# Fixed expert blocks, an adding scatter, and the first blocks beside the last batch's routing

## The chip, the cores and the metric

The kernel runs on one core of one Trainium2 chip. The metric is the device time of one execution in microseconds, and lower is better. A core has five engines that work side by side, each in the order of its own instructions: TensorE (PE, matrix products), VectorE (DVE), ScalarE (ACT), GpSimd (POOL) and SyncE (SP, which here only issues transfers). Transfers run on 16 DMA engines that all queues share. An engine waits for another, or for a transfer, through semaphores, and everything behind a waiting instruction on the same engine waits too.

## The reference

The input `x` is 4 images of 32 x 32 positions with 256 channels, so 4 batches of 1024 tokens. Layer 0 is a convolution with a selective scan. Layer 1 is an attention without a softmax over tokens, followed by a mixture of 16 experts, of which each token takes two:

```
t = tokens(layer0(x))
t = t + attn(layernorm(t))
xe = layernorm(t)                                  # 4096 x 256
probs = softmax(xe @ gate_w + gate_b)              # 16 experts
top_probs, top_idx = top_k(probs, 2); top_probs /= sum(top_probs)
hidden = silu(xe @ w1[e]) * (xe @ w2[e])           # 256 -> 512
t = t + sum over the two experts e:  top_prob * (hidden @ w3[e])   # 512 -> 256
```

The reference computes every expert for every token and weights most of them with zero. The kernel computes only the two that count.

## The kernel before, in words

**Layer 0** (to line 1159) takes most of the time: a scan over 64 states for each of 4 batches, with all engines busy. The change does not touch it.

**Attention** (lines 1221 to 1742) runs batch by batch in an order written out by hand. The iteration for batch `o` multiplies out its attention, prepares the keys and queries of batch `o + 1`, and does the routing of batch `o - 1`. The routing is a generator, `route`, whose steps are small DVE operations; `on_with(steps, n)` puts the next `n` of them at a given place in the order. For the last batch nothing follows to run its routing beside, so lines 1730 to 1742 put it at the end: `turn_e` turns the normalised tokens `xe`, `gates` multiplies them by the gate weights, `turn_g` turns the result back, and `route` picks the two experts, counts for each token how many earlier tokens chose the same expert, and writes the one-hot matrices `qh` of the place in a block. The tokens themselves are written to a DRAM tensor `xd` by `expert_in`. They stay in SBUF too, in `t_all`.

**Blocks.** The expert stage works on blocks of 128 (token, choice) pairs that share one expert. Lines 1748 to 1825 lay the blocks out once all four batches are routed: each expert gets the number of blocks that its count needs, one expert after the other. `eid` holds the expert of each block, `src` the row of `xd` for each place of each block, and `dst` the row of the output list. To find `src` and `dst`, each of 64 groups of 128 pairs is multiplied (bf16) by a matrix that marks its block.

**The expert stage** (lines 1830 to 1931) runs `NFULL` = 74 blocks, and more only under a condition on the number that is used. For each block, `fetch_in` reads the expert number into a register on SP and loads `w1` and `w2` (0.5 MB each), `fetch_out` loads `w3` (0.5 MB), both four blocks ahead, and POOL gathers 128 rows of `xd` with an indirect transfer. `turn_rows` transposes the rows on PE, `hidden` computes half of the hidden layer into PSUM (tile `p12`, four buffers), SiLU on ACT, the product on DVE, and `result` multiplies by `w3`. `put_result` copies the block's result to `yb` (four buffers) and POOL scatters it with an indirect transfer to `yd`, a DRAM list with one row for each (token, choice) pair. POOL's queue therefore alternates gathers and scatters.

**The end** (lines 1934 to 1947). Because the two results of a token lie in two rows of `yd`, the last loop loads all of `yd` (8 loads of 1 MB), multiplies each row by its weight `wts`, adds it to `t_all` on DVE, and stores the output from ACT's queue.

The lines that set the order at the border and in a block:

```
            hidden(i, 0)                    # lines 1917 to 1925, for each block i
            result(i - 1, 2); put_result(i - 1)
            turn_rows(i + 1)
            hidden(i, 2)
            result(i, 0)
```

Of the kernel before, what the change touches and what calls it, by code (L numbers as in the profile page):

```python
# [8 lines left out]
F32 = mybir.dt.float32  # L9
# [7 lines left out]
P = 128  # L17
BANK = 512

BS = P  # L20
# [13 lines left out]
def conv_ssm_attn_moe_kernel(ctx: ExitStack, tc: tile.TileContext, a: dict, out: bass.AP):  # L34
# [19 lines left out]
    NBLK = 2 * NB * L // BS + NE - 1  # L54
    assert 2 * NS == P
# [1112 lines left out]
    wts = l1.tile([P, 2, NTA], F32, name="wts")  # L1168

    t_all = l1.tile([P, NTA, C], F32, name="t_all")  # L1170
    xd = dram.tile([NB * L, C], F32, name="xd")

    yd = dram.tile([2 * NB * L + P, C], F32, name="yd")
# [4 lines left out]
    groups_f = l1.tile([P, NTA], F32, name="groups_f")  # L1178

    places = l1.tile([P, BS], BF16, name="places")  # L1180
    blocks_h = l1.tile([P, NBLK], BF16, name="blocks_h")

    groups = l1.tile([P, NTA], BF16, name="groups")
    part_pk = l1.tile([P, 2], F32, name="part_pk")
    spare = l1.tile([P, 1], F32, name="spare")
# [7 lines left out]
    counts = [l1.tile([P, NE], F32, name=f"counts{b}") for b in range(NB)]  # L1193
    within = l1.tile([P, 2, NTA], F32, name="within")
    qh = l1.tile([P, 2, NTA, BS], BF16, name="qh")

    def constants(first):
        def count(t, n, lo, step=1, across=0):
            nc.gpsimd.iota(
                t, [[step, n]], base=lo, channel_multiplier=across,  # L1200
                allow_small_or_imprecise_dtypes=True,
            )

        if first:
            count(iota, NE, NE)
            make_upper_triangular(nc, before, 1.0, diag=False)
            count(places_f, BS, 0)
            count(blocks, NBLK, 0)
            count(groups_f, NTA, 0)
            count(part_pk, 2, 1, 1, 2)  # L1210
            count(spare, 1, 2 * NB * L + 1, 1, 1)
            count(block_p, 1, 0, 1, 1)
        else:
            nc.vector.memset(every, 1.0)
            nc.vector.memset(keep, 1.0)
            nc.vector.memset(keep[:, :, 0:1], 0.0)
            nc.vector.tensor_copy(places, places_f)
            nc.vector.tensor_copy(blocks_h, blocks)
            nc.vector.tensor_copy(groups, groups_f)

    with tc.tile_pool(name="wa", bufs=1) as wa, tc.tile_pool(name="att", bufs=1) as att, \
            tc.tile_pool(name="sm", bufs=2) as sm, \
            tc.tile_pool(name="ps_b", bufs=2, space=PSUM) as ps_b, \
            tc.manual_schedule():
        HT = NT // 2
        tbs = [t_all[:, b * NT : (b + 1) * NT, :] for b in range(NB)]
        for i in (0, HT):
            nc.sync.dma_start(out=tbs[0][:, i : i + HT, :], in_=rows(td, 0)[:, i : i + HT, :])
        for b in range(1, NB - 1):
            nc.sync.dma_start(out=tbs[b], in_=rows(td, b))  # L1230
        nc.sync.dma_start(out=tbs[-1][:, TPB:, :], in_=rows(xf, NB - 1)[:, TPB:, :])
        nc.sync.dma_start(out=tbs[-1][:, :TPB, :], in_=rows(td, NB - 1)[:, :TPB, :])
        wg = load_rows("L1_ffn_gate_w", CK, NE, wa)
        gb = load_bcast("L1_ffn_gate_b", NE, wa)
        wqk, wvo, bqk, bvo, bout = made["mats"]

        batch = [{} for _ in range(NB)]

        def stat(on, kind, x, i, n=NT):

            if i == 0:
                on[kind] = (
                    sm.tile([P, n, 2], F32, name="ln_mv", tag=kind + "mv"),
                    sm.tile([P, n], F32, name="ln_rs", tag=kind + "rs"),
                )
            st = sm.tile([P, 6], F32, name="ln_st", tag="ln_st", bufs=4)
            nc.vector.bn_stats(st, x[:, i, :])
            nc.vector.bn_aggr(on[kind][0][:, i, :], st)

        def root(on, kind, lo, hi):  # L1250

            mv, rs = on[kind]
            nc.scalar.activation(rs[:, lo:hi], mv[:, lo:hi, 1], AF.Sqrt, bias=eps5)
            nc.vector.reciprocal(rs[:, lo:hi], rs[:, lo:hi])

        def turned(x, dst, half, put):

            for ck in range(CK):
                ps = ps_b.tile([P, BANK], F32, name="ps_t", tag="pt")
                for i in range(HT):  # L1260
                    nc.tensor.transpose(ps[:, blk(i, P)], x(half * HT + i)[:, blk(ck, P)], ident)
                put[ck](dst[:, ck, blk(half)], ps)

        on_both = (nc.scalar.copy, nc.vector.tensor_copy)


        ysb = made["ysb", len(units) - 1]
        last = {}

        def last_turn(j):  # L1270
            ps = ps_b.tile([P, BANK], F32, name="ps_l", tag="pt")
            for m in range(DK):
                nc.tensor.transpose(ps[:, blk(m, P)], ysb[:, j, blk(m, P)], ident)
            last["yT", j] = sm.tile([P, BANK], F32, name="yT")
            nc.scalar.copy(last["yT", j], ps)

        def last_product(j):
            if j % 2 == 0:
                last["po"] = ps_b.tile([P, 2, C], F32, name="po_l", tag="po")
            last["po", j] = last["po"][:, j % 2, :]  # L1280
            for m in range(DK):
                nc.tensor.matmul(
                    last["po", j], last["yT", j][:, blk(m, P)], w_o[:, m, :],
                    start=(m == 0), stop=(m == DK - 1),
                )

        def last_sum(j):
            t = tbs[-1][:, TPB + j, :]
            nc.gpsimd.tensor_tensor(t, t, b_o, ALU.add)
            nc.vector.scalar_tensor_tensor(  # L1290
                t, last["po", j], last["ln1"][1][:, j : j + 1], t, ALU.mult, ALU.add
            )


        def scaled(b, lo, hi):
            if lo == 0:
                batch[b]["xh"] = att.tile([P, NT, C], F32, name="xh", bufs=2)
            for i in range(lo, hi):
                nc.scalar.activation(
                    batch[b]["xh"][:, i, :], tbs[b][:, i, :], AF.Copy,  # L1300
                    scale=batch[b]["ln2"][1][:, i : i + 1],
                )

        def turn_x(b, half):
            if half == 0:
                batch[b]["xhT"] = att.tile([P, CK, L], F32, name="xhT", bufs=2)
            turned(lambda i: batch[b]["xh"][:, i, :], batch[b]["xhT"], half, on_both if b == 0 else (nc.vector.tensor_copy,) * 2)

        def qk(b, i):
            on = batch[b]  # L1310
            if i == 0:
                on["sq"] = att.tile([P, NT, 2, C], F32, name="sq")
                on["sums"] = sm.tile([P, NT, 2], F32, name="sums")
                on["q4"] = sm.tile([P, NT], F32, name="q4")
            pqk = ps_b.tile([P, 2, C], F32, name="pqk", tag="pq", bufs=3)
            for ck in range(CK):
                nc.tensor.matmul(
                    pqk.rearrange("p s c -> p (s c)"), on["xhT"][:, ck, blk(i, P)],
                    wqk[:, ck, :], start=(ck == 0), stop=(ck == CK - 1),
                )  # L1320
            t = sm.tile([P, 2, C], F32, name="qk")
            nc.vector.tensor_tensor(t, pqk, bqk.rearrange("p (s c) -> p s c", s=2), ALU.add)
            for k in range(2):
                nc.scalar.activation(
                    on["sq"][:, i, k, :], t[:, k, :], AF.Square,
                    accum_out=on["sums"][:, i, k : k + 1],
                )
            nc.gpsimd.tensor_tensor(tbs[b][:, i, :], tbs[b][:, i, :], bout, ALU.add)

        def fourth(b, i):  # L1330
            on = batch[b]
            junk = sm.tile([P, C], F32, name="junk", bufs=1)
            nc.scalar.activation(
                junk, on["sq"][:, i, 0, :], AF.Square, accum_out=on["q4"][:, i : i + 1]
            )

        def k2(b, half):

            on = batch[b]
            lo, hi = half * HT, (half + 1) * HT  # L1340
            if half == 0:
                on["k2"] = att.tile([P, NT, C], F32, name="k2")
                on["ksq"] = att.tile([P, NT, C], F32, name="ksq")
                on["fold"] = sm.tile([P, 2, C], F32, name="fold", bufs=1)
            rk = sm.tile([P, HT], F32, name="rk")
            nc.vector.tensor_scalar(rk, on["sums"][:, lo:hi, 1], 1e-7, None, ALU.add)
            nc.vector.reciprocal(rk, rk)
            for i in range(lo, hi):
                nc.scalar.activation(
# [631 lines left out]
```

## Time and profile before

| | |
|---|---|
| median of 3 runs | 3436.63 us (3435.61 to 3440.5) |
| profiled execution, its own time | 3446.1 us |
| its span in the profile | 3444.3 us |
| busy share of the span | PE 92%, DVE 84%, ACT 79%, POOL 77% |
| mean DMA rate over the span | 101 GB/s |
| weight loads of the expert stage | 222 of 512 KB, median 6.0 us from issue to landing |
| gathers `xb` | 74, median 5.6 us to landing |
| scatters `yd` | 74, median 5.2 us to landing |

The busy shares are means over stages of different kinds. The scan of layer 0 ends at about 2690 us of the span. What the change touches lies in the last 750 us, and is best read by stretches:

| stretch, us | what runs | PE busy, us | DMA, GB/s |
|---|---|---|---|
| 2690 to 2927 | attention, routing of batches 0 to 2 beside it | 207.95 of 237 | 12 to 75 |
| 2927 to 2974 | routing of batch 3, layout of the blocks | 14.97 of 47 | 162 |
| 2974 to 3399 | 74 expert blocks | 413.02 of 425 | 304 |
| 3399 to 3444 | outputs gathered and summed | 2.66 of 45 | 287 |

In the lines that follow, `L1901` is line 1901 of the kernel before, `x16` a number of instructions, and the square brackets give how long the engine had stood idle and what released it. PE's products are f32 here, and one product of the program appears as two instructions.

### The profile page before, as it was taken

What the parts mean: (1) busy time and instruction counts of PE and PEld (TensorE: products, weight loads), DVE (VectorE), ACT (ScalarE), POOL (GpSimd) and SP (SyncE); (2) the same over time, 40 slices, a digit from 0 to 9 for tenths busy, and PEclk for the clock granted to TensorE, in tenths of its full rate; (3) what the DMA queues carried; (4) which work ended last, traced back from release to release, by engine and by line L of the source; (5) the groups of instructions that cost most, each with busy time, mean ns of one, the idle gap of its engine ahead of it and who ended that gap; (6) DMA issues with size and microseconds to landing.
All of it is one profiled execution on the core that took longest, in us unless ns stands there. A gap on an engine that the chain in (4) does not pass through costs nothing. (4 is left out here: it accounts for less than half of the span.)

```text
span 3444.3 us, 63146 instructions
## 1 busy us (share of the span) xinstructions
PE 3180.6 (92%) x23385; PEld 2757.0 (80%) x23385; DVE 2882.1 (84%) x3302; ACT 2714.7 (79%) x4611; POOL 2662.0 (77%) x1141
## 2 busy tenths in 40 slices
PE   7899999999999999999999999899999888699995
PEld 4588988988898988889988887688777566598894
DVE  4699999999999999999999999999999676422224
ACT  1699999999999999999999999999999444221110
POOL 0389998999999989999998999999899541133331
PEclk9999999999999999999999999999999999899997
DMA  3542223224232422243323225222122100799996
GB/s 103 151 68 64 67 68 67 71 70 67 66 76 67 75 69 71 65 57 84 72 68 71 67 65 75 57 62 65 57 65 65 53 19 25 243 327 310 317 313 227
DMA packets 442665, 348.59 MB, mean 101 GB/s; under 512 B 221153, under 2 KB 328929, under 8 KB 442354
## 3 DMA queue, kind: packets, MB, share of 16 engines
q1 hardware_dynamic: 422882, 320.74, 35.1%
q0 software_dynamic: 7104, 19.41, 1.7%
q10 hardware_dynamic: 12368, 4.37, 0.5%
q8 instruction: 187, 3.06, 0.4%
q14 instruction: 124, 1.02, 0.1%
HBM read 310.11 MB, written 33.78 MB: 100 GB/s over the span
## 5 line engine op out<-in xcount | busy, mean ns | idle before, releaser
L957 POOL TENSOR_TENSOR h<-h,cb_n 128x2048 f32<-128x2048 f32 x512 | 2146.4, 4200 | 134.5 <-DVE h L950 91.2
L924 ACT ACTIVATE da<-dt,l_conv_a_log_sb 128x512 f32<-128x512 f32 x2048 | 1435.4, 712 | 25.4 <-DVE h L950 24.4
L904 ACT ACTIVATE bx<-dtxT,proj 128x512 f32<-128x512 f32 x1748 | 1244.0, 712 | 29.6 <-DVE dtxT L596 17.0
L971 PE MATMUL y<-ident,h 128*128 128x128 f32 x8192 | 1238.0, 274 | 8.8 <-POOL h L957 5.8
L950 DVE TENSOR_TENSOR_SCAN h<-da,last,ps 128x512 f32<-128x512 f32 x1024 | 1218.0, 1269 | 6.8 <-PE ps L936 1.7
L950 DVE TENSOR_TENSOR_SCAN h<-da,ps 128x512 f32<-128x512 f32 x1024 | 1170.3, 1203 | 37.7 <-ACT da L924 9.7
L936 PE MATMUL ps<-ident,bx 128*128 128x128 f32 x6992 | 1118.0, 275 | 41.8 <-DVE h L950 28.7
L971 PEld LDWEIGHTS y<-ident,h 128*128 128x128 f32 x8192 | 980.4, 141 | 99.4 <-issue 20.3
L936 PEld LDWEIGHTS ps<-ident,bx 128*128 128x128 f32 x6992 | 819.1, 142 | 101.6 <-DVE h L950 80.1
L1887 DVE TENSOR_TENSOR hT<-s,p 128x256 f32<-128x256 f32 x148 | 62.4, 422 | 338.3 <-ACT s L1886 338.3
L1881 PE MATMUL p<-xT,w 128*128 128x128 f32 x2368 | 291.8, 277 | 0.5 <-ACT xT L1870 0.5
L1881 PEld LDWEIGHTS p<-xT,w 128*128 128x128 f32 x2368 | 285.0, 194 | 4.7 <-ACT xT L1870 0.9
L936 PE MATMUL ps<-ident,bxp 128*128 128x128 f32 x800 | 237.6, 297 | 53.6 <-DVE h L950 41.0
L1901 POOL DMA_INDIRECT yd<-yb,dst x74 | 73.0, 987 | 266.8 <-DMA yd<-yb,dst 161.0
L1886 ACT ACTIVATE s<-p 128x256 f32<-128x256 f32 x148 | 56.7, 383 | 275.0 <-PE p L1881 275.0
L409 PE MATMUL bg<-pad,dgc 128*128 128x256 f32 x864 | 258.2, 380 | 0.5 <-DMA dgc<-diags 0.5
L936 PEld LDWEIGHTS ps<-ident,bxp 128*128 128x128 f32 x800 | 112.0, 140 | 139.1 <-DVE h L950 84.2
L931 PE MATMUL ps<-dgb,dtxT 128*128 128x128 f32 x800 | 171.0, 296 | 22.0 <-DMA dgb<-diag_b 9.7
L915 POOL TENSOR_SCALAR bxp<-dtxT,proj 128x512 f32<-128x512 f32 x200 | 140.6, 703 | 60.5 <-DVE dtxT L596 60.5
L931 PEld LDWEIGHTS ps<-dgb,dtxT 128*128 128x128 f32 x800 | 120.8, 191 | 48.9 <-DVE h L950 35.2
L1893 PE MATMUL pf<-w,hT 128*128 128x256 f32 x592 | 152.5, 380 | 0.1
L1850 POOL DMA_INDIRECT xb<-xd,src x74 | 71.9, 972 | 96.5 <-DMA w<-in_L_ffn_w_dram 72.4
(310 smaller groups left out, 2435.5 us busy)
## 6 DMA issues: line engine op xcount, KB each, us to landing
cb_n<-cd SPq DMA_DIRECT2D x512, 256.0 KB, 3.3
w<-in_L_ffn_w_dram SPq DMA_DIRECT2D x222, 512.0 KB, 6.0
dgc<-diags SPq DMA_DIRECT2D x84, 192.0 KB, 3.1
diag_b<-zero SPq DMA_DIRECT2D x2, 4096.0 KB, 16.8
y<-yd SPq DMA_DIRECT2D x8, 1024.0 KB, 10.1
dgb<-diag_b SPq DMA_DIRECT2D x100, 64.0 KB, 3.1
last<-h SPq DMA_DIRECT2D x256, 2.0 KB, 3.0
xd<-xe SPq DMA_DIRECT2D x8, 512.0 KB, 2.9
```

The costliest lines, as they stand in the source:

```text
L409: nc.tensor.matmul(made["bg"].rearrange("p (h w) -> p h w", w=WW)[:, blk(c, deep), :], made["dgc", m * 3 + i][:, j, :], pads[m][:, at : at ...
L904: nc.scalar.activation(t, made["dtxT", u][:, j, :], AF.Copy, scale=made["proj", u][:, j, R + n : R + n + 1])
L915: nc.gpsimd.tensor_scalar(t, made["dtxT", u][:, 0, :], made["proj", u][:, 0, R + n : R + n + 1], 1.0, ALU.mult, ALU.mult,)
L924: nc.scalar.activation(t, made["dt", u][:, m, :], AF.Exp, scale=A[:, m, n : n + 1])
L931: nc.tensor.matmul(t[:, blk(j, P)], made["dtxT", steps[s][0]][:, j, blk(m, P)], made["dgb", s], start=True, stop=True,)
L936: nc.tensor.transpose(t[:, blk(j, P)], made["bx", s, j][:, blk(m, P)], ident)
L950: nc.vector.tensor_tensor_scan(h[:, m, 1:], made.pop(("da", s, m)), made.pop(("dbx", s, m)), 0.0 if seg == 0 else last[b][:, n, m : m + 1] ...
L957: nc.gpsimd.tensor_tensor(h[:, :, :BANK], h[:, :, 1:], over_middle(made["c", s], DK), ALU.mult)
L971: nc.tensor.matmul(made["y", u][j][:, blk(m, P)], made["h", s][:, m, blk(j, P)], ident, is_transpose=True, start=n == 0 and m == 0, stop=n ...
L1881: nc.tensor.matmul(p12[:, j, s, :], on[w, i][:, ck, blk(h + j, P)], on["xT", i][:, ck, :], start=(ck == 0), stop=(ck == CK - 1),)
L1893: nc.tensor.matmul(on["pf", i], on["hT", i][:, hk, :], on["w3", i][:, hk, :], start=(hk == 0), stop=(hk == HK - 1),)
L1901: nc.gpsimd.indirect_dma_start(yd[:, :], bass.IndirectOffsetOnAxis(dst[:, i : i + 1], 0), yb, None)
```

## The change

**Fixed blocks.** Each of the 16 experts gets three blocks whether it fills them or not (`FIX` = 3, so `NFIX` = 48), and 25 further places (`NFULL` now means these) are dealt to the experts that need more; beyond that, a conditional part runs. Which block a pair goes to is known, for the first three blocks of its expert, as soon as its own batch is routed. `route` therefore adds each batch's part of the fixed blocks' contents to `found` (a comparison and a product on DVE, one more operation on ACT, 16 bf16 products on PE). The further places are laid out by `more_places` and `more_rows`, with 64 smaller bf16 products.

**The first blocks.** The first block of each of experts 0 to 7 (`SOON` = 8) is filled from batches 0 to 2 only: `floors` lifts the count from which batch 3's tokens of these experts go on to at least 128. These eight blocks are computed first, and the routing of the last batch is turned into a generator, `rest_of_routing`, whose steps, followed by the layout of the other blocks, are put into the block loop: three after each half block for the first eight blocks, then one. The routing of batch 2 runs at twice its pace to be done in time. `w1`, `w2` and `w3` of the very first block are loaded during the last batch's attention.

**The adding scatter.** Each row of `xd` is two numbers longer and carries the two weights of its token, written by a transfer of 8 bytes for each token. `weigh` picks the right one, `put_result` multiplies the block's result by it, and POOL's indirect transfer adds the rows to the output in DRAM. Before that, the attention's result is written to the output batch by batch from ACT's queue. `yd` and the last loop are gone. A place of a block that no token fills gathers a row of zeros and must add it somewhere: `nonmembers`, `count_them`, `place_them` and `list_them` make, for each expert, a table of tokens to which such places point, so that no row occurs twice in one transfer.

**Weights.** An expert's three fixed blocks (two for experts 0 to 7) follow each other and share one load. `wp` has two buffers instead of six, and two more lie in the space of `t_all`, which is now three tiles that are free once they are written out (`spare`). PSUM for the expert stage is smaller too: `ps_h` has two buffers instead of four, `ps_x` one instead of two, as the routing's pool `ps_c` stays open.

```diff
-    NBLK = 2 * NB * L // BS + NE - 1
+    FIX = 3
+    NFIX = FIX * NE
+    SOON = NE // 2
+    NMORE = 2 * NB * L // BS - 2 * (FIX - 1)
+    NBLK = NFIX + NMORE
...
+    none = sm.tile([P, C + 2], F32, name="none_t", tag="junk", bufs=1)
+    nc.gpsimd.memset(none, 0.0)
+    nc.sync.dma_start(out=xd[NB * L :, :], in_=none)
     for i in (0, HT):
         nc.sync.dma_start(out=tbs[0][:, i : i + HT, :], in_=rows(td, 0)[:, i : i + HT, :])
...
+        with nc.allow_non_contiguous_dma(reason="two weights a token"):
+            nc.sync.dma_start(
+                out=rows(xd, b)[:, :, C:], in_=wts[:, b * NT : (b + 1) * NT, :]
+            )
...
+        nc.vector.tensor_tensor(
+            ih, over_middle(blocks_h[:, :NFIX], 2 * NT),
+            over_last(at.rearrange("p k g -> p (k g)"), NFIX), ALU.is_equal,
+        )
...
+        pf = ps_c.tile([P, 2, NFIX], F32, name="pf_r", tag="po")
+        for k in range(2):
+            for i in range(NT):
+                nc.tensor.matmul(
+                    pf.rearrange("p s n -> p (s n)"), qh[:, k, b * NT + i, :],
+                    code[:, k * NT + i, :2, :].rearrange("p s n -> p (s n)"),
+                    start=(k + i == 0), stop=(k == 1 and i == NT - 1),
+                )
...
+        if n is None:
+            on_with(steps, 40)
+            sources(0, SOON, found[:, 0, :SOON], found[:, 1, :SOON])
+            given_rows.update(range(SOON))
+            for key in soon[:3]:
+                fetch_rows(key)
+        out(o, 7)
+        nc.scalar.dma_start(out=rows(of, o), in_=tbs[o])
...
     def put_result(key):
         yb = ffn.tile([P, C], F32, name="yb", bufs=4)
+        nc.vector.tensor_scalar(yb, on_b["pf", key], on_b["wt", key], None, ALU.mult)
+        c = key[0]
         nc.gpsimd.indirect_dma_start(
-            yd[:, :], bass.IndirectOffsetOnAxis(dst[:, i : i + 1], 0), yb, None
+            of[:, :], bass.IndirectOffsetOnAxis(dst[:, c : c + 1], 0), yb, None,
+            compute_op=ALU.add,
         )
...
+        load_ahead(0, 0)
+        look_ahead(0, AHEAD)
+        turn_rows(todo[0])
+        for i in range(n + 1):
+            if i < n:
+                look_ahead(i, AHEAD + 1)
+                hidden(todo[i], 0)
+            on_with(beside, 3 if i < fast else 1)
+            if i > 0:
+                result(todo[i - 1], 2)
+                put_result(todo[i - 1])
+            load_ahead(i, i)
+            if i + 1 < n:
+                turn_rows(todo[i + 1])
+            if i < n:
+                hidden(todo[i], 2)
+                weigh(todo[i])
+                result(todo[i], 0)
+            on_with(beside, 3 if i < fast else 1)
...
+    def rest_of_routing():
+        o = NB - 1
+        turn_e(o, 0)
+        yield
         gates(o, 0)
         turn_e(o, 1)
+        yield
         gates(o, 1)
+        yield
         turn_g(o)
+        yield
+        yield from route(o)
+        yield
+        sources(SOON, NFIX, found[:, 0, SOON:], found[:, 1, SOON:])
+        given_rows.update(range(SOON, NFIX))
+        yield
...
-    with tc.tile_pool(name="fin", bufs=4) as fin:
-        ofs = of.rearrange("(q g p) c -> q p g c", p=P, g=TPB)
-        yds = yd[: 2 * NB * L, :].rearrange("(q g p k) c -> q p g k c", p=P, g=TPB, k=2)
-        for q in range(NTA // TPB):
-            y = fin.tile([P, TPB, 2, C], F32, name="y")
-            nc.sync.dma_start(out=y, in_=yds[q])
...
-            nc.scalar.dma_start(out=ofs[q], in_=t_all[:, q * TPB : (q + 1) * TPB, :])
```

The early blocks' `choices`, `one_block` and `targets` (which weight a place takes, and where its row goes) stand after out(3, 7). `load_ahead` loads the weights of up to four blocks ahead as far as the two buffers of each home are free, in the order of the blocks; `look_ahead` issues gathers up to five ahead as soon as the rows are known. `place_them` stands at the start of the last batch's iteration, `list_them` before out(3, 5).

## The prediction

> **What bounds the kernel now.** I read the page, then a table of stretches cut at the stage borders, the waits of the expert stage, the order of time at its two ends, and the chain of waits.
>
> The stretches (columns: stretch, its length, then busy us and instruction count of PE, PE weight loads, DVE, ACT, POOL; granted clock; DMA share; GB/s):
>
> ```profile
> 2880.00:2927.00 47.00, 39.25 (x188) 28.46 (x186) 33.34 (x105) 18.39 (x45) 8.41 (x7) 1.00 0.08 29
> 2927.00:2974.00 47.00, 14.97 (x94) 9.62 (x95) 32.50 (x81) 11.35 (x15) 5.00 (x5) 0.69 0.46 162
> 2974.00:3399.00 425.00, 413.02 (x3096) 389.73 (x3097) 93.02 (x220) 85.04 (x222) 138.43 (x142) 0.99 0.91 304
> 3399.00:3444.00 45.00, 2.66 (x14) 1.75 (x13) 26.53 (x66) 0.38 (x1) 1.55 (x2) 0.57 0.78 287
> ```
>
> The last quarter has two holes in TensorE's work: 47 us of routing before the experts (15 us busy) and 45 us of gathering the outputs after them (under 3). Between them 425 us of expert blocks are bound twice over: PE 97% busy, DMA at 304 GB/s. Whatever is taken off the DMA there can win no more than PE's 12 idle us; the holes are worth far more.
>
> The timeline gives PE's own pace inside a block and, on POOL, what runs beside it:
>
> ```profile
> 3050.26 0.99 POOL L1901 DMA_INDIRECT yd<-yb,dst  x1 [4.31 <-DMA yd<-yb,dst]
> 3050.63 1.95 PE L1881 MATMUL p<-xT,w 128*128 128x128 f32 x16
> ...
> 3056.15 1.95 PE L1881 MATMUL p<-xT,w 128*128 128x128 f32 x16
> 3057.26 0.99 POOL L1901 DMA_INDIRECT yd<-yb,dst  x1 [4.74 <-DVE yb L1900]
> ...
> 3061.68 1.95 PE L1881 MATMUL p<-xT,w 128*128 128x128 f32 x16
> 3063.44 0.99 POOL L1901 DMA_INDIRECT yd<-yb,dst  x1 [3.92 <-DMA yd<-yb,dst]
> ```
>
> The second products of successive blocks begin 5.52 us apart, the scatters of their results 7.0 and 6.2. So the scatters already run slower than PE here, covered by the four `yb` buffers. Waits of the stage (total us, times, longest), and the line of the scatter:
>
> ```profile
> POOL yd L1901 <- DMA yd<-yb,dst: 161.0, 44, 5.3
> PE px L1868 <- DMA xb<-xd,src: 20.1, 14, 8.6
> ...
> DMA to landing us min/median/max: 2.4/5.2/7.7
> ```
>
> Each scatter waits for the one before to land. PE's stalls are gathers which are late because POOL stood behind a scatter. POOL's scatter chain is thus the nearest limit after PE, and the one that the change touches.
>
> The ends of the stage, from the timeline:
>
> ```profile
> 2943.02 0.80 PE L1546 MATMUL pc<-hot,every_t 128*128 128x128 f32 x2 [6.49 <-DVE hot L1540]
> ...
> 2975.05 3.75 PE L1881 MATMUL p<-xT,w 128*128 128x128 f32 x16 [0.51 <-ACT xT L1870]
> ...
> 3402.46 0.97 POOL L1901 DMA_INDIRECT yd<-yb,dst  x1 [2.87 <-DVE yb L1900]
> 3407.16 18.80 SPq L1939 DMA_DIRECT2D y<-yd  x8
> 3412.81 15.92 DVE L1943 SCALAR_TENSOR_TENSOR t_all<-y,wts,t_all 128x256 f32<-128x256 f32 x40 [10.63 <-DMA y<-yd]
> ```
>
> The first expert product begins at 2975.05; the last scatter is issued at 3402.46, and 41.8 us pass from there to the end of the span.
>
> **What the Trainium skill says.** "DMA: Bandwidth & Descriptors", section "SWDGE vs HWDGE vs iDMA": accumulating in a DMA is for GpSimd's queue only. So it stays where the plain scatter is. The same page, "Rules for kernel authors": the accumulate reads its destination and writes it later with nothing held in between, so one must wait for the earlier DMA's semaphore. Two experts of one token add to one row, so the chain of scatters stays serial, as it is in this trace (the 161.0 us). The page's "Latency and other measured facts" puts an HBM access at 0.2 us on average and 2 us at high load. The trace has no accumulate; its plain scatter lands in 2.4 us at best and 5.2 at the median, a spread that fits that row.
>
> **The change, part by part.** The sum is made on the profiled execution (span 3444.3, time 3446.1); that is 9.5 us over the median of 3436.63, and I take the difference off the median.
>
> *Attention, batches 0 to 2.* Each batch's routing gains a comparison and a product over 16x48 bf16 (the row of L1795 has 1471 ns for 1264 elements, so 0.9 us each), an addition, and 16 bf16 products into `found` (the 64 of L1806 took 4.39 + 2.68 = 7.07 us, so 0.11 each, 1.8 us). PE is 84 to 95% busy here and DVE 64 to 75%: +2 us for each of the first two routings; at nothing they would hide in PE's idle share, at most 4. On SP the clearing of `xd`'s last rows stands ahead of the loads of `tbs[0]` and waits for a memset on POOL, whose last scan product ends at 2688.7; those loads were issued at 2684.4, so they are 5 us late. ScalarE's first use of them was held until 2700.7 by its own queue (DVE had finished at 2695.2), so most is covered: +2, between 0 and 5. The writes of `tbs` to the output go at times with the DMA at 29 GB/s. They stand on ACT, which at the last batch border was idle for 6.80 us. `place_them` is 32 small operations on POOL, which is 18% busy there. Total +6 us, ends 0 and 13.
>
> *The start of the blocks.* DVE is what the last batch waits for: it runs almost without a gap from 2909 to 2933.5, where the third routing ends. Before `sources(0, 8)` it loses out(3, 7) and its root (1.5 us) and gains about 3.2 (two passes of 0.9, five small ones of 0.2, the rest): 2935.3, with the wait for `found` 2936. `list_them` (32 small products, about 4 us) fits under this. The gather: 0.3, 1.2 to issue, some 3 to land without weights beside it (minimum 2.9), and 1.2 from the transposes to the product: 2942, against 2975.05. With the 6 us: 2948. Ends: 2940, and 2965 if the gather takes its loaded 6.2 us and DVE is later.
>
> *The blocks.* 73 instead of 74. The reference's own logits give 73 filled blocks, 48 of them fixed and exactly 25 more, so the conditional part stays out. 73 x 5.52 = 403.0.
>
> *Routing beside them.* Its PE work goes on: turning and gates of the last batch 2.1 + 3.8 + 0.8, counts 0.8, `found` 1.8, the 64 products of `more_rows` 7.1, rest 1.3: 17.7 us. Its latency was the hole. Three steps stand after each half block and in the order of every engine; PE waits behind them for ACT's copies (about 3), for the two switches of ACT's table (1.28 each), for DVE's `qh` (2), and SiLU and `hT` of the blocks stand behind these on ACT and DVE: 7 us. Step 26 of 48 lists the fixed blocks' rows in block 4, and block 8's gather is issued in block 5, two and a half blocks ahead. On SP the last batch's 8-byte weights wait for the gathers already issued, weight loads stand behind them, and later gathers on POOL wait for them; they come in block 2, four blocks ahead of use. Block 1's weights are the first in memory that attention leaves: issued behind the second half of `xe` at about 2944 (+6), 1.5 MB at 330 GB/s in 4.8 us and 2 to land; PE needs them 5.5 after the start: 3 us of stall. Together 10, ends 4 and 30.
>
> *The scatter.* Weights fall from 74 to 49 loads of three (16 of these are one per expert, 8 for the early blocks, 25 for the rest): 111 MB to 77 over the same time. The adding scatter moves its row once more and reads before it writes. Its period is issue plus landing, with some 0.7 us around. Lower end: a plain scatter with no weights beside it, 3.8 us (3394.78 to 3398.62 to 3402.46 in the trace): PE's pace holds. Upper end: the loaded 7.0 of above and 2 us for a read at high load, 9. Loads will be in flight about half the time. I take 1 us more than the plain scatter: 7.5 loaded, 4.5 unloaded, mean near 5.9. PE's pace after block 8 is 5.52 + 0.11; 65 x 0.22 = 14 us (the kernel before lost 424 - 74 x 5.52 = 15.5).
>
> *The end.* Gone: eight loads of 1 MB, 64 sums, eight stores. Left after PE's last product: 0.7 to the scatter, 4.3 to land (3402.46 to 3406.76), 1 for the addition, 4.6 to close (3439.7 to 3444.3): 10.6.
>
> Sum: 2948 + 403 + 17.7 + 10 + 14 + 10.6 = 3403; 41 below 3444.3. On the median: **3396 us**.
>
> **Rivals.**
> *Scatter hidden, borders free.* The lower scatter cost and half of the 16 us for attention and stalls: 22 us less, 3374. For it: unloaded scatters of 3.8 us, a third fewer weight bytes. Against: the chain lagged at 6.2 to 7.0.
> *The adding scatter becomes the bound.* One mechanism: POOL waits for each addition to land, `yb` fills, DVE holds the result, PE stops. The first is issued near 2954; 72 periods, then 10.6. It decides above 5.63 us and cancels the whole gain at (3444.3 - 2954 - 10.6) / 72 = 6.66. At 7.5: 3505, so 3497 us, slower. For it: 6.2 to 7.0 without any addition. Against: those were taken at 0.98 DMA share.
> *The early start is spent.* Block 0 begins, but weights, rows and the routing chain leave PE waiting through the first eight: 30 for the 10 and 2953 for 2948, so 3421. For it: the routing was 47 us of almost pure latency. Against: rows are listed four blocks ahead.
> *The change doesn't do what it says*, if one expert's count fell in another block and 35 conditional blocks ran, near 190 us: the nearest counts are 3 and 5 off a border; under 1 in 100.
>
> **How the numbers follow.** Forecast 0.48 (3380 to 3416), hidden scatter 0.18, spent start 0.10, scatter as bound 0.24. Of the last, periods of 6.66 to 7.1 give up to 3470, about half. Range 3360 to 3470. A difference of 0.2% (7 us; three runs spread by 4.9) is the least that a measurement of this kernel can tell: faster 0.74, same 0.03, slower 0.23.
>
> **What would show it.** First expert product at 2940 to 2960 and PE without a hole of 47 us; the period of the adding scatter (below 5.6, or above 6.6 with PE waiting at `yb` or `xb`); DMA rate near 230 to 260 GB/s after block 8; about 11 us from the last product to the end. I am wrong if additions land in over 6 us with weights beside them most of the time, or if PE stands over 30 us in the first eight blocks.

## The result and the profile after

| | median, us | runs | range, us |
|---|---|---|---|
| before | 3435.64 | 6 | 3432.97 to 3440.5 |
| after | 3421.64 | 6 | 3416.79 to 3426.93 |

The ratio is 0.9959, with a 95% interval of 0.9947 to 0.9972: faster by 14 us, where the forecast had 41. The profiled execution of the kernel after took 3419.33 us, with a span of 3417.6.

The two profiled spans differ by 26.7 us, but 9.0 of these lie in layer 0, which the change does not touch: its last product of states starts on POOL at 2684.5 us before and at 2675.5 after. So times are taken from that point, called S, in what follows. A landing is the time from the start of a transfer's issue until it has arrived; the period is the time from one scatter's issue to the next.

| from S, us | before | forecast | after |
|---|---|---|---|
| S to the first expert product | 290.5 | 263.5 | 263.9 |
| to the first product of block 8 (counted from 0) | | 71.9 | 75.6 |
| to PE's last product | | 372.8 | 381.9 |
| both of these: all blocks | 426.7 | 444.7 | 457.5 |
| PE's last product to the end of the span | 42.6 | 10.6 | 20.7 |
| sum | 759.8 | 718.8 | 742.1 |

The two holes shrank, by 26.6 us at the start and 21.9 at the end. The blocks take 30.8 us more than before, 18.0 of them foreseen. The forecast is 23.3 us short from S on, of which 19.2 lie in the blocks after the eighth and in the end. The table of stretches of the kernel after, cut at its own borders (the columns are those of the prediction's table):

```profile
2901.00:2939.00 38.00, 21.14 (x116) 16.57 (x115) 26.39 (x89) 6.09 (x14) 13.41 (x18) 0.77 0.22 66
2939.00:3015.00 76.00, 60.09 (x455) 52.00 (x455) 40.41 (x151) 21.98 (x46) 20.93 (x17) 0.94 0.74 222
3015.00:3397.00 382.00, 364.33 (x2733) 343.13 (x2732) 101.83 (x329) 73.62 (x194) 159.22 (x123) 1.00 0.72 205
3397.00:3418.00 21.00, 0.00 (x0) 0.00 (x0) 0.42 (x1) 0.00 (x0) 4.66 (x3) 0.55 0.18 23
```

PE has no long hole any more at the start. From block 8 on it is idle for 17.7 of 382 us, where in the stage before it was 12 of 425, although the DMA share fell from 0.91 to 0.72 and the rate from 304 to 205 GB/s. So fewer bytes move and PE still waits more. In the last 21 us there are three POOL instructions and the rest of one copy on DVE.

What PE waits for is found in two steps. The waits from 3015 to 3397 us have a single line for PE's products, and the waits from 2940 on have the scatter's (total us, times, longest). The view of the scatter's source line gives its issue (ns: least, median, most) and its landing:

```profile
PE px L2040 <- DMA xb<-xd,src: 17.5, 14, 3.4
```

```profile
POOL out_dram L2086 <- DMA out_dram<-yb,dst: 124.8, 37, 5.7
```

```profile
L2086 POOL DMA_INDIRECT out_dram<-yb,dst x73: 1552/1587/1635, 2960.1 to 3406.7; - x73
...
DMA to landing us min/median/max: 3.7/4.9/8.0
```

PE's waits from block 8 on are late gathers, as they were before, and account for its idle time (17.5 of 17.7 us). Gathers are late because they stand on POOL behind a scatter which waits for the one before to land: 37 of the 73 are put down to that, for 124.8 us together. POOL's timeline shows the alternation:

```profile
3092.88 1.59 POOL L2086 DMA_INDIRECT out_dram<-yb,dst  x1 [3.61 <-DVE wt L2051]
3094.77 0.99 POOL L1811 DMA_INDIRECT xb<-xd,src  x1 [0.30 <-issue]
3100.56 1.59 POOL L2086 DMA_INDIRECT out_dram<-yb,dst  x1 [4.80 <-DMA out_dram<-yb,dst]
3102.45 0.99 POOL L1811 DMA_INDIRECT xb<-xd,src  x1 [0.30 <-issue]
3106.68 1.59 POOL L2086 DMA_INDIRECT out_dram<-yb,dst  x1 [3.25 <-DVE hT L2069]
3108.58 0.99 POOL L1811 DMA_INDIRECT xb<-xd,src  x1 [0.30 <-PE p L2062]
3113.30 1.59 POOL L2086 DMA_INDIRECT out_dram<-yb,dst  x1 [3.74 <-DMA out_dram<-yb,dst]
```

The scatters start 7.7, 6.1 and 6.6 us apart, and the gathers with them, while PE's pace would be 5.5. The third is put down to `hT`, which is no operand of it. The chain of waits over these microseconds, in order of time (start, us, what), settles what it waited for:

```profile
3092.88 6.89 DMA out_dram<-yb,dst
...
3100.56 5.33 DMA out_dram<-yb,dst
...
3106.68 5.83 DMA out_dram<-yb,dst
```

The landing of the second ends at 3105.89, and the third is issued 0.79 us later, the same distance as between the first landing (3099.77) and the second issue. So a link of this chain, from one scatter's issue to the next, is a landing and 0.79 us, and nothing but landings sets the pace here. From the eighth scatter to the last, over 65 links, the period is 5.970 us. The two ends of the stage, from the timeline:

```profile
2938.21 0.69 PE L2040 MATMUL px<-ident,xb_s 128*128 128x128 f32 x2 [7.46 <-DMA xb_s<-xd,src]
2939.44 3.78 PE L2062 MATMUL p<-xT,w 128*128 128x128 f32 x16 [0.54 <-ACT xT L2042]
...
3396.93 0.48 DVE L2084 TENSOR_SCALAR yb<-pf,wt 128x256 f32<-128x256 f32 x1 [0.96 <-PE pf L2077]
3397.63 1.55 POOL L2086 DMA_INDIRECT out_dram<-yb,dst  x1 [3.03 <-DVE yb L2084]
3402.15 1.55 POOL L2086 DMA_INDIRECT out_dram<-yb,dst  x1 [2.97 <-DMA out_dram<-yb,dst]
3406.75 1.55 POOL L2086 DMA_INDIRECT out_dram<-yb,dst  x1 [3.04 <-DMA out_dram<-yb,dst]
```

The last block's result is copied at 3396.93 and scattered at 3406.75: two others stand in front of it. With little else in flight (23 GB/s in the last stretch) they still come 4.5 and 4.6 us apart.

### The profile page after: what moved, and what is told of

The parts are those of the page before. It is cut to its first block, busy times and chain, and to the rows that moved or that the text cites. A ratio compares the mean times of both kernels' runs of the same rounds, so it can differ in the third digit from the quotient of the medians.

```text
span 3417.6 us, 62769 instructions
## 1 busy us (share of the span) xinstructions
PE 3175.0 (93%) x23450; PEld 2754.6 (81%) x23450; DVE 2889.6 (85%) x3462; ACT 2716.9 (79%) x4624; POOL 2731.8 (80%) x1176
## 5 line engine op out<-in xcount | busy, mean ns | idle before, releaser
L928 ACT ACTIVATE da<-dt,l_conv_a_log_sb 128x512 f32<-128x512 f32 x2048 | 1437.8, 714 | 20.7 <-DVE h L954 19.7
L954 DVE TENSOR_TENSOR_SCAN h<-da,ps 128x512 f32<-128x512 f32 x1024 | 1169.9, 1202 | 31.3 <-ACT da L928 9.1
L2086 POOL DMA_INDIRECT out_dram<-yb,dst x73 | 115.8, 1586 | 257.1 <-DMA out_dram<-yb,dst 124.8
L2062 PE MATMUL p<-xT,w 128*128 128x128 f32 x1440 | 177.5, 277 | 0.5 <-ACT xT L2042 0.5
L2062 PEld LDWEIGHTS p<-xT,w 128*128 128x128 f32 x1440 | 172.8, 193 | 3.2 <-ACT xT L2042 0.9
L413 PEld LDWEIGHTS bg<-pad,dgc 128*128 128x128 f32 x864 | 130.5, 191 | 1.1 <-DMA dgc<-diags 1.1
L2062 PE MATMUL p<-xT,m 128*128 128x128 f32 x896 | 111.4, 278 | 0.0
```

Source lines behind the costliest of these rows:

```text
L413: nc.tensor.matmul(made["bg"].rearrange("p (h w) -> p h w", w=WW)[:, blk(c, deep), :], made["dgc", m * 3 + i][:, j, :], pads[m][:, at : at ...
L928: nc.scalar.activation(t, made["dt", u][:, m, :], AF.Exp, scale=A[:, m, n : n + 1])
L954: nc.vector.tensor_tensor_scan(h[:, m, 1:], made.pop(("da", s, m)), made.pop(("dbx", s, m)), 0.0 if seg == 0 else last[b][:, n, m : m + 1] ...
L2062: nc.tensor.matmul(p12[:, j, s, :], w_of(w, key)[:, ck, blk(h + j, P)], on_b["xT", key][:, ck, :], start=(ck == 0), stop=(ck == CK - 1),)
L2086: nc.gpsimd.indirect_dma_start(of[:, :], bass.IndirectOffsetOnAxis(dst[:, c : c + 1], 0), yb, None, compute_op=ALU.add,)
```

## The experiments

The theory was: the chain of additions, each waiting for the landing of the one before, sets the pace after block 8 and the end; what makes a link long is the weight loads beside it. The rivals: PE or the gathers lose time for another reason (fewer buffers in PSUM and for weights, the smaller steps of the routing that remain in the loop), or the overlap of the last routing with the first blocks costs as much as it saves.

Three of the runs repeat the kernels as they are, so that the others have a profile and a median from the same chip beside them.

> The kernel before, unchanged, for a second profile. Theory (the profiled execution of before had a slow layer 0, which the change does not touch): the last product of the states on POOL, at 2684.5 us in the first profile, comes at 2675 to 2680, and the rest to the end of the span stays near 759.8 us. Rival (the extra 10 us of that execution lay in the part that the change replaces): the product again comes near 2684, and the rest is shorter than 755.

> The changed kernel, unchanged, as the base of this batch: 3417 to 3427 us; from the last product of the states on POOL to the end 742 us, within 4.

The kernel before took 3449.43 us in this one execution, 757.6 of them from S (759.8 in the first profile). S came at 2690.1, not at 2675 to 2680: the first profile was not unusually slow in layer 0. The 23 further executions on this chip have a median of 3441.97. The kernel after took 3435.32, ratio 0.9985 (0.9975 to 0.9994), with 751.0 us from S, a scatter period of 6.051 and a landing of 5.2 at the median; the time and the 751.0 us lie above what was expected. In a second set, on another chip:

> The changed kernel once more, as the base of this batch: from the last product of the states on POOL to the end of the span 742 to 751 us, PE's blocks after the eighth at 5.83 to 5.93 us each.

3432.9 us, ratio 0.9968 (0.9958 to 0.9978), 752.7 us from S, 5.87 for each of PE's blocks, period 6.055. By the three ratios the gain is 14, 5 and 11 us. The period in these two profiles is 0.08 us longer than in the first, which is worth 65 x 0.08 = 5 us.

**The addition left out.** The scatter writes its rows instead of adding them.

```diff
             of[:, :], bass.IndirectOffsetOnAxis(dst[:, c : c + 1], 0), yb, None,
-            compute_op=ALU.add,
         )
```

> The addition is left out of the scatter: each block's rows overwrite the output rows, so the output lacks the sum. Theory (the adding scatter's price sets its period, mean 6.0 us after block 8): issue falls from 1.59 us to about 0.99, the landing by 0.5 to 1.5, the period to PE's pace of 5.52, and 13 to 20 us go: 3402 to 3409. Rival (the period is set by the wait for a landing beside the weight loads, whatever it does): issue falls by 0.6, the landing hardly, and under 8 us go: 3414 or more.

3396.15 us, ratio 0.9871 (0.9854 to 0.9887): 39.2 us less than the kernel after beside it, more than the 13 to 20 expected; 10.6 of them are the end alone (9.2 us after PE's last product, where the kernel after beside it has 19.8). The same stretch of 340 us in the middle of the expert stage, of the kernel after in its first profile and, in the next fence, of this run (the columns are those of the stretches above):

```profile
3040.00:3380.00 340.00, 322.49 (x2424) 303.99 (x2423) 89.89 (x289) 65.64 (x173) 142.66 (x111) 0.99 0.76 218
```

```profile
3040.00:3380.00 340.00, 340.00 (x2587) 324.25 (x2586) 95.97 (x308) 70.32 (x186) 117.47 (x120) 1.00 0.69 228
```

PE does not stop once in this stretch. Its own pace is 5.495 us for a block. Smaller PSUM, fewer weight buffers and the steps in the loop are all still there, so none of them is what PE waits for. The scatters still wait for one another (25 times, for 90.7 us), but their links are short enough. That leaves the addition, but not whether its length or its order does it.

**Two targets.** Every second block adds into another DRAM tensor, `yd2`, which is filled with the attention's result like the output. Nothing of an addition is saved; only the next one does not wait for it.

```diff
+    yd2 = dram.tile([NB * L, C], F32, name="yd2")
...
+        nc.scalar.dma_start(out=rows(yd2, o), in_=tbs[o])
...
+        n_put[0] += 1
         nc.gpsimd.indirect_dma_start(
-            of[:, :], bass.IndirectOffsetOnAxis(dst[:, c : c + 1], 0), yb, None,
+            (of if n_put[0] % 2 else yd2)[:, :], bass.IndirectOffsetOnAxis(dst[:, c : c + 1], 0), yb, None,
             compute_op=ALU.add,
```

> The adding scatters go in turn to the output and to a second DRAM tensor, so that each waits only for the last but one; every second block's result is missing in the output, as the two tensors are not added up. Theory (the serial wait for the landing holds PE): no wait for the last scatter, period at PE's 5.52, 65 blocks in about 360 us instead of 382, no lag of two scatters at the end: 15 to 25 us less, 3397 to 3407. Rival (the stalls are late gathers and weights, or the DMA engines' own share): less than 6 us.

3404.0 us, ratio 0.9892 (0.9876 to 0.9909), 31.3 us less than the kernel after beside it, where 15 to 25 were expected. The stretch, and then the waits of the scatters from 3010 us on:

```profile
3040.00:3380.00 340.00, 340.00 (x2587) 324.29 (x2588) 95.96 (x310) 69.82 (x184) 156.10 (x121) 1.00 0.77 226
```

```profile
POOL out_dram L2090 <- DVE yb L2087: 98.0, 33, 8.2
POOL yd L2090 <- DVE yb L2087: 96.5, 34, 4.7
```

The issue still takes 1.57 us on the mean, the DMA moves as much as in the kernel after (226 against 218 GB/s), and PE is busy throughout. The scatters now wait for results, not for each other. So PE was held neither by POOL's time nor by the bandwidth that the addition takes, but by the serial order of the landings. From the last product to the end 11.5 us are left, so about 9 of the 20.7 were the queue of two scatters. What is still missing here is the merge of `yd2`, which would have to read and add 4 MB at the end; what is left of the 31.3 us with it is not shown.

**Weights taken away.** The 25 further blocks multiply by whatever their buffers hold and load nothing.

```diff
+        if c >= NFIX:
+            n = weights["spare"] = weights["spare"] + 1
+            for name in ("w1", "w2", "w3"):
+                weights[name, key] = (
+                    spare[2][:, n % 2] if name == "w3" else spare[n % 2][:, int(name == "w2")]
+                )
+            return True
```

> The weights of the 25 further blocks are not loaded; these blocks use what lies in their buffers, so their part of the output is not computed. Every scatter, addition and product stays. Theory (an addition lands late because weight loads are in flight beside it, 6.5 to 8 us against 3.8): median landing below 4.5, period at PE's 5.5, 22 to 32 us less than the base. Rival (the addition is slow by itself): the landing keeps its median near 5, under 10 us less.

3405.86 us, ratio 0.9889 (0.9856 to 0.9921): 27.0 less than the kernel after in this set, as expected (22 to 32). The stretch, and the view of the scatters:

```profile
3040.00:3380.00 340.00, 340.00 (x2590) 324.27 (x2589) 96.19 (x310) 70.12 (x185) 154.94 (x120) 1.00 0.49 113
```

```profile
DMA to landing us min/median/max: 3.7/3.9/8.5
```

The chain is as serial as before, but with about half the bytes beside it (113 GB/s for the 215 of the kernel after in this set) the median landing falls from 5.3 us there to 3.9, and the chain no longer limits: blocks come every 5.495 us. With half the traffic beside it the addition is affordable; under the full load it is not. The gathers, too, have less traffic beside them here, but in the two runs before they had all of it, and PE did not wait for them.

**More buffers.** If the chain were short enough on the mean and only uneven, deeper buffers would help.

```diff
-            t = on_b["ffn"].tile([P, C + 2], F32, name="xb", bufs=6)
+            t = on_b["ffn"].tile([P, C + 2], F32, name="xb", bufs=10)
...
-        yb = ffn.tile([P, C], F32, name="yb", bufs=4)
+        yb = ffn.tile([P, C], F32, name="yb", bufs=8)
...
-                look_ahead(i, AHEAD + 1)
+                look_ahead(i, AHEAD + 4)
```

> Eight buffers for the results instead of four, ten for the gathered rows instead of six, and gathers issued up to eight blocks ahead. Theory (the serial additions are the bound, buffers only move the wait): PE runs at 5.5 us a block, but the last scatter is issued no more than 8 us earlier, and the lag at the end grows from 9 us to 20 or more: 0 to 8 us less than the base. Rival (the stalls are made by too few buffers and gathers behind a waiting scatter): 15 us or more less.

3432.97 us, ratio 0.9974 (0.9962 to 0.9985): the same as the kernel after beside it (3432.9), as expected (0 to 8 less). Two views, the stretch and POOL's timeline after PE's last product at 3396.81, show where the gain went:

```profile
3040.00:3380.00 340.00, 332.68 (x2512) 315.87 (x2511) 93.62 (x300) 68.46 (x180) 139.94 (x109) 0.99 0.77 224
```

```profile
3397.78 1.55 POOL L2086 DMA_INDIRECT out_dram<-yb,dst  x1 [2.92 <-DVE yb L2084]
3402.27 1.55 POOL L2086 DMA_INDIRECT out_dram<-yb,dst  x1 [2.93 <-DMA out_dram<-yb,dst]
3406.73 1.55 POOL L2086 DMA_INDIRECT out_dram<-yb,dst  x1 [2.91 <-issue]
3411.29 1.55 POOL L2086 DMA_INDIRECT out_dram<-yb,dst  x1 [3.01 <-DMA out_dram<-yb,dst]
3415.87 1.55 POOL L2086 DMA_INDIRECT out_dram<-yb,dst  x1 [3.02 <-DMA out_dram<-yb,dst]
3420.34 1.55 POOL L2086 DMA_INDIRECT out_dram<-yb,dst  x1 [2.92 <-DMA out_dram<-yb,dst]
```

PE wins ten of its idle microseconds back (332.68 busy for 322.78 in the profile of the kernel after of this set), and six scatters are left when it ends, where there were three. The end grows from 23.3 to 34.2 us. The period of the chain is 5.997 us, for 6.055 in the kernel after of this set; from S the last scatter is issued 5.2 us earlier in these two profiles, of which the medians show nothing (the profiled execution of this set's kernel after was the longest of its 17). Here buffers move a wait that the chain causes; they hardly shorten the chain.

**The routing first.** All steps of the last batch's routing and of the layout are put ahead of the first block.

```diff
         look_ahead(0, AHEAD)
+        on_with(beside, 99)
         turn_rows(todo[0])
```

> All steps of the last batch's routing and of the layout are put ahead of the first block instead of beside the first eight; weights and gathers of the first blocks are issued before. Theory (laying it beside the blocks hides its latency): the first eight blocks fall from about 80 us to 48, a hole of 45 to 60 us opens before them, 12 to 28 us more in all than the base. Rival (in the engines' own order the steps stall the blocks as much as they hide): within 6 us of the base.

3447.48 us, ratio 1.0017 (1.0005 to 1.003), 14.6 more than the kernel after beside it (12 to 28 were expected). The first expert product comes 307.7 us after S instead of 263.9, and PE stands again, as the stretch ahead of that product shows:

```profile
2940.00:2997.00 57.00, 22.19 (x149) 13.52 (x146) 36.57 (x143) 14.79 (x30) 6.31 (x6) 0.62 0.51 162
```

The first eight blocks (from the first product to the copy of the eighth result) then take 48.9 us instead of 83.8. The overlap therefore moves the start by 43.8 us and gives 34.9 of it back inside these blocks. To the end of the span, 7.5 us are left in the profiles (760.2 from S for 752.7) and 14.6 in the medians. The overlap pays, but most of the hole was only displaced: PE's routing products and the steps' waits come along.

## Why the forecast was right in direction and wrong in size

**The start** held. From S the forecast had the first gather issued after 257.8 us and the first product after 263.5; the trace has 257.8 (2933.29) and 263.9. Inside it two estimates were off without effect: `place_them`, which I took for small, is 25.4 us of POOL (32 operations of 812 ns at the median), and `list_them`, put at 4 us, takes 0.9 on PE. Both lay beside other work. The 6 us for attention are inside this sum and were not measured alone, so an agreement to 0.4 us is better than its parts can answer for.

**The first eight blocks** cost 31.4 us over PE's pace, with 27.7 forecast. Two errors cancel in part there, which is luck: PE is idle for 15.5 of the 75.6 us, for the 10 forecast, and the other 15.9 are the routing's products, for 17.7. PE's longest waits from 2939 to 3015 us, again total, times, longest, are steps of the routing:

```profile
PE one L2228 <- ACT code L2223: 5.3, 6, 1.6
PE one L2183 <- DVE ef L2181: 3.2, 1, 3.2
PE pf_r L1652 <- DVE qh L1644: 3.0, 2, 2.7
PE pc L1574 <- DVE hot L1568: 2.1, 1, 2.1
```

These four, 13.6 us, are PE's waits for ACT's copies and DVE's one-hots that the forecast had priced at about 7 with the table switches; the wait for the weights of block 1, priced at 3, is not among them. The rival "early start is spent" asked for 20 more in the stalls and 5 in the start; that did not come, and that its 3421 us are the measured median is chance.

**The blocks after the eighth and the end** are where the forecast failed: the term "65 x 0.22 = 14" for the adding scatter, and the end of 10.6 that assumed the last scatter to follow its result at once. The mechanism was named rightly: the chain of additions stays serial, waits for landings, and delays gathers. Its two sizes were close as well: 4.5 unloaded was 4.5 to 4.6, and the mean period near 5.9 was 5.970. The 4.5 was partly luck. The plain scatters 3.8 us apart, from which it starts, waited for results, as the line at 3402.46 says (`yb`); the same trace has links of 3.2 us, and the addition costs 1.3 more than those, not 1. The 7.0 of the loaded end was one of two links that were read; from the eighth scatter to the last of the kernel before the period is 5.64 us. What failed is what I made of the two sizes, in two ways.

- The excess was counted above 5.63, that is PE's 5.52 and a 0.11 that the forecast does not explain and that no term of its sum charges to these blocks, and the 0.22 stands for a period of 5.85. A chain that bounds is compared with the pace that is in the sum: 65 x (5.97 - 5.52) = 29 us, not 14. Of the 15 between, 7 are the 0.11 and 8 the step from 5.85 to 5.97.
- The excess does not only stop PE. With four `yb` buffers a part of it waits in the queue and comes out after the last product; the forecast put this at nothing. Measured, 23.1 us lie in the blocks (381.9 less 65 x 5.52) and about 9 in the end (20.7, with 11.5 in the run with two targets): 32 together, where the sum had 14.

Of the forecast's own signs two told of this: 20.7 us from the last product to the end for about 11, and 205 GB/s from block 8 on for 230 to 260. The others did not: a period of 5.97 lies between the two marks, 5.6 and 6.6, and the median landing of 4.9 us is below the 6 at which I called myself wrong. (The fall of the weight loads from 111 MB to 77 mixes two units; in the unit of the first it is 73.5.)

The page "DMA: Bandwidth & Descriptors" of the Trainium skill, section "Latency and other measured facts", gives an access to HBM, the DRAM in which `xd` and the output lie, 0.2 us on average and 2 us at high load. The runs agree in direction (a median landing of 5.3 us, and 3.9 with the weights taken away), but the landings of the kernel after spread from 3.7 to 8.0 us, and these 4.3 us are more than one such access explains. The same holds for the plain scatter of the kernel before, which the forecast called a fit: 2.4 to 7.7 us.

**The rivals.** "The adding scatter becomes the bound" described what happened: the period passed its point of decision, 5.63. It did not cancel the gain, as its second point, 6.66, was not reached; but that point was wrong too. It spread the loss over all 72 periods from the first scatter on, while the first eight are paced by the routing (5.5 to 11.1 us apart). Counted over the 65 that the chain rules, the remaining 17.7 us would be gone at 5.97 + 17.7 / 65 = 6.24. The two later profiles, at 6.051 and 6.055, lie nearer to it, and their gains are the smaller ones. "Scatter hidden" is what the run with the plain scatter comes close to: 46 us less than the kernel before on its chip, where that rival had 63.

**The rest of the difference.** From S on the sum missed by 23.3 us, in the medians by 25.6. The 2.3 between them come from resting the sum on one execution of each kernel: the profiled one lay 9.5 us over the median before and 2.3 under it after, and in layer 0, up to S, they differ by 9.0.

That the chain, and its length under load, holds back the expected gain was shown by three runs that each remove one thing (addition, order, about half of the load) and each free PE. Which part of a landing grows under load was not taken apart.

## What to carry to other kernels

A chain of dependent transfers is priced as a second engine: its period under the traffic that will run beside it, against the pace that stands in the sum, times the links it rules, and the links still queued when the work ends are added to the end. In this case more buffers only decided on which side of the last product that price was paid; independent targets (their merge left out), or less traffic beside the chain, removed it. And when a hole is closed by running its work beside something else, count what comes along: here 34.9 of 43.8 us.

## What the runs showed of the hardware

Adding costs GpSimd more time at the issue, which I had not foreseen: 1.59 us for each indirect transfer (the view of L2086 above) against 0.99 for the plain one of the same rows, in the run without the addition:

```profile
L2086 POOL DMA_INDIRECT out_dram<-yb,dst x73: 969/987/1008, 2971.6 to 3387.5; - x73
```

As a landing is counted from the start of its issue, these 0.6 us lie in every link. That is more than the 0.48 by which the period of 5.970 exceeds PE's 5.495, so by this estimate a shorter issue alone would have let the chain keep pace; no run shortened it alone. On the software queue the packets double while the bytes stay (queue, packets, MB, share of the engines; the kernel after, then the run without the addition):

```profile
q0 software_dynamic: 14016, 19.22, 3.1%
```

```profile
q0 software_dynamic: 7008, 19.22, 1.7%
```

With little traffic beside them, links that waited for a landing are 4.5 us long with the addition and 3.2 without (the kernel before, with 41 GB/s in this link); 0.6 of these 1.3 us are the issue:

```profile
3387.81 0.98 POOL L1901 DMA_INDIRECT yd<-yb,dst  x1 [2.23 <-DVE yb L1900]
3390.99 0.97 POOL L1901 DMA_INDIRECT yd<-yb,dst  x1 [2.20 <-DMA yd<-yb,dst]
```

Among weight loads the longest links that waited for a landing are 8.6 us in the kernel after (336 GB/s during that link) and 8.8 in the run without the addition (274 GB/s), so what makes the longest ones long is not the addition.

Executions of unchanged code differ by more than the effect of many an edit: in the three profiles of the kernel after, S lay at 2675.5, 2684.0 and 2692.1 us (the third on another chip than the second). The mean granted clock of TensorE over the span was 0.987, 0.981 and 0.979 in them. The kernel before in the second set shows the same tendency: 13 executions at 0.982 or more have a median of 3438.2 us, 15 at 0.979 or less 3444.4. What ties the two is not shown.
